# Two cross-attention layers on one core: K's PSUM banks emptied by one ScalarE copy each, masked copies of K made by GpSimd from SBUF

## The chip, the cores and the metric

The kernel runs on one core of a Trainium2 chip. The core's engines run side by side, each through its own queue of instructions: PE (TensorE, the matmuls; PEld is its weight load), DVE (VectorE), ACT (ScalarE), POOL (GpSimd) and SP (SyncE, which issues most DMAs here). They wait for each other through semaphores. The metric is the time of one execution on the device, in microseconds (us).

## The reference

Two layers of multi-head cross-attention, one after the other, each with a residual. There are 32 batch elements with 256 queries of 320 channels, and 77 context rows of 512 channels; 20 heads of 16 channels. All is float32. Further key and value weights of the reference belong to context rows that don't exist in this case, and have no effect.

```python
def layer(x, ctx, Wq, Wk, Wv, Wo, bo):           # x (32, 256, 320), ctx (32, 77, 512)
    q, k, v = heads(x @ Wq), heads(ctx @ Wk), heads(ctx @ Wv)      # 20 heads of 16
    s = einsum('bhqd,bhkd->bhqk', q, k) / sqrt(16)
    o = einsum('bhqk,bhkd->bhqd', softmax(s, axis=-1), v)
    return merge(o) @ Wo + bo + x
x = layer(x, ctx, ...)     # first layer's weights
x = layer(x, ctx, ...)     # second layer's
```

## The kernel before

**Units.** A unit is one layer of one pair of batch elements: 16 pairs x 2 layers = 32 units. Channels lie in the partitions. The 20 heads of the two elements make five groups (g = 0 to 4); in a group, 128 partitions hold four blocks of 32 channels, each of them two heads of 16 (e = 0 and 1). So that one head of a block can be used without its neighbour, K is kept twice, each time with the other head's channels multiplied by zero: `kT[:, e, g]`. `masks` holds the two patterns of ones and zeros. `kM` is kT plus `less`, which puts -1 into one row of the masked half; in the scores that row meets a row of q into which the query's maximum has been written, so that the maximum is subtracted by the matmul itself.

**Steps of a unit.** `keys` and `keys_rest` project K (psk_0 and psk_1 with groups 0 to 3, psk_2 with group 4). `queries` and `queries_rest` project Q, which ACT copies to SBUF; a DMA doubles it (L277). `vals` projects V. `maxima(u, g)` multiplies queries by kT into four banks psm (L326), and DVE takes their maxima (L334); `turn` transposes them and eight DMAs write them into q (L347). `scores(u, g)` multiplies kM by q into four banks pss (L360), and ACT takes the exponential (L366). `products` multiplies by V into po (L380). `divide` transposes po on DVE (L392), takes reciprocals (L396) and normalizes on POOL (`normal`, L401); `turn_back` transposes that on DVE (L415). `finish` and `finish_rest` project the output into psy, and DVE adds bias and residual (L422).

**Order.** The order is written out by hand. Time is cut into slots, five to a unit; unit u's slots begin at s = 5u, and each step is given a slot and a place in it. With u-8 for slot s - 8 and so on, the steps that matter here are:

```python
order = ("load", "maxima", "turn", "scores", "values", "rest", "back", "full", "last")
at(s - 8 if u else s - 9, "rest", lambda u=u: keys(u))
at(s - 7, "rest", lambda u=u: keys_rest(u))
at(s - 5, "rest", lambda u=u: queries_rest(u))
at(s - 6 + g, "maxima", lambda u=u, g=g: maxima(u, g))
at(s + g, "scores", lambda u=u, g=g: scores(u, g))
```

In every slot PE thus does the maxima of one group of a later unit, the scores of one group of the present one, the products of the group before, and then some projection. Each engine runs its instructions in program order.

**Banks.** All matmul outputs come from one pool of eight PSUM banks, `bank(name)`, used in turn: the ninth allocation gets the first one's bank, and its first matmul waits until the last reader of that bank is done. In SBUF, kT and kM have three buffers each (`bufs=3`).

**Who empties K's banks before.** psk_0 and psk_1: one DVE multiply each, which writes both masked copies (L229). psk_2: two ACT activations with the mask as their scale (L253). After these, two POOL additions make kM from kT (L256).

Of the kernel before, what the change touches and what calls it, by code (L numbers as in the profile page):

```python
# [48 lines left out]
F32 = mybir.dt.float32  # L49
AF = mybir.ActivationFunctionType  # L50
ALU = mybir.AluOpType
AX = mybir.AxisListType

B, S, C, CA, L = 32, 256, 320, 512, 77
HEADS, HD = 20, 16
P = 128
# [4 lines left out]
NG = 5  # L61
# [29 lines left out]
def xattn_kernel(ctx: ExitStack, tc: tile.TileContext, xT, cT, cP, weights, outT):  # L91
    nc = tc.nc
# [3 lines left out]
    work = ctx.enter_context(tc.tile_pool(name="work", bufs=3))  # L96
# [6 lines left out]
    def bank(name):  # L103
        return psum.tile([P, 512], F32, tag="bank", name=name)
# [55 lines left out]
    masks = const.tile([P, 2], F32, name="masks")  # L160
    nc.vector.tensor_reduce(masks, r32.rearrange("p (e d) -> p e d", d=HD), AX.X, ALU.add)

    less = const.tile([P, 2], F32, name="less")
# [4 lines left out]
    st = [{} for _ in units]  # L168

    def by_columns(out, lhsT, rhs, **flags):  # L170

        for m in range(0, out.shape[0], 32):
            nc.tensor.matmul(out[m : m + 32], lhsT[:, m : m + 32], rhs, **flags)  # L173

    def of_group(x, g):

        if g < 4:
            return x[:, (g // 2) * NT + (g % 2) * S : (g // 2) * NT + (g % 2 + 1) * S]
        return x[:, 2 * NT : NX]
# [21 lines left out]
    def project_rest(ps, w, w22, x):  # L201

        for kc in range(3):
            for i in range(4):
                b, m = i // 2, i % 2
                r = slice(32 * i, 32 * i + 32)
                if kc < 2:
                    lhsT = w[:, kc, 2 * P + 32 * m : 2 * P + 32 * m + 32]
                    rhs = x[:, kc * NT + b * S : kc * NT + (b + 1) * S]
                else:  # L210
                    lhsT, rhs = w22[:, 0, r], x[:, 2 * NT : NX]
                nc.tensor.matmul(ps[r, 0:S], lhsT, rhs, start=(kc == 0), stop=(kc == 2))  # L212


    def keys(u):
        p, layer = units[u]
        w, c_sb = w_sb[layer], cs[u]
        kT = st[u]["k"] = work.tile([P, 2, NG, L], F32, tag="kT", name=f"kT_{u}", bufs=3)
        for t in range(2):
            ps = bank(f"psk_{u}_{t}")  # L220
            for kc in range(NKA):
                by_columns(
                    ps[:, 0 : 2 * L],
                    w["k"][:, kc, t * P : (t + 1) * P],
                    c_sb[:, kc, :],
                    start=(kc == 0),
                    stop=(kc == NKA - 1),
                )
            nc.vector.tensor_tensor(  # L229
                kT[:, :, 2 * t : 2 * t + 2].rearrange("p e g k -> p e (g k)"),  # L230
                ps[:, 0 : 2 * L].unsqueeze(1).broadcast_to([P, 2, 2 * L]),
                masks.unsqueeze(2).broadcast_to([P, 2, 2 * L]),
                ALU.mult,
            )

    def keys_rest(u):

        p, layer = units[u]
        w, c_sb = w_sb[layer], cs[u]
        kT = st[u]["k"]  # L240
        ps = bank(f"psk_{u}_2")
        for kc in range(NKA):
            for i in range(4):
                b, m = i // 2, i % 2
                nc.tensor.matmul(  # L245
                    ps[32 * i : 32 * i + 32, 0:L],
                    w["k"][:, kc, 2 * P + 32 * m : 2 * P + 32 * m + 32],
                    c_sb[:, kc, b * L : (b + 1) * L],
                    start=(kc == 0),
                    stop=(kc == NKA - 1),  # L250
                )
        for e in range(2):
            nc.scalar.activation(kT[:, e, 4], ps[:, 0:L], AF.Copy, scale=masks[:, e : e + 1])  # L253
        kM = st[u]["km"] = work.tile([P, 2, NG, L], F32, tag="kM", name=f"kM_{u}", bufs=3)
        for e in range(2):
            nc.gpsimd.tensor_scalar_add(kM[:, e], kT[:, e], less[:, e : e + 1])  # L256

    def queries(u):
        p, layer = units[u]
# [10 lines left out]
    def queries_rest(u):  # L270
        p, layer = units[u]
        w = w_sb[layer]
        q0, q1 = st[u]["q"]
        ps = bank(f"psq_{u}_2")
        project_rest(ps, w["q"], w["q22"], xs[p])
        nc.scalar.copy(of_group(q0, 4), ps[:, 0:S])
        nc.sync.dma_start(out=q1, in_=q0)  # L277

    def load_chunk(layer, i):
        n = min(P, B * L - i * P)  # L280
        c_sb = cvs[layer, i] = io.tile([P, NKA, P], F32, tag="cv", name=f"cv_{layer}_{i}", bufs=3)
        nc.sync.dma_start(out=c_sb[:, :, :n], in_=cT[:, :, i * P : i * P + n])
# [170 lines left out]
    for u, (p, layer) in enumerate(units):  # L453
# [3 lines left out]
        if u > 0:  # L457
            at(s - 12, "load", lambda u=u: load_context(u))
        at(s - 8 if u else s - 9, "rest", lambda u=u: keys(u))
        at(s - 9, "last", lambda u=u: queries(u))  # L460
        at(s - 7, "rest", lambda u=u: keys_rest(u))
        need = range(p * NB * L // P, ((p + 1) * NB * L - 1) // P + 1)
        when = s - 6
        for i in need:
# [6 lines left out]
            made[layer] += 1  # L471
            when = s - 5
        at(s - 5, "rest", lambda u=u: queries_rest(u))
        for g in range(NG):
            at(s - 6 + g, "maxima", lambda u=u, g=g: maxima(u, g))
# [121 lines left out]
```

## Time and profile before

| | |
|---|---|
| median of 3 runs | 999.02 us (992.94 to 1000.55) |
| the profiled execution's own time | 995.15 us |
| its span, first to last instruction | 993.4 us |
| PE busy | 977.5 us, 98% |
| DVE busy | 590.9 us, 59% |
| ACT busy | 421.7 us, 42% |
| POOL busy | 182.7 us, 18% |
| DVE multiply from psk_0, psk_1 (L229) | 64 instructions, 479 ns each |
| ACT activation from psk_2 (L253) | 64 instructions, 322 ns each |
| POOL addition for kM (L256) | 64 instructions, 1260 ns each |

Busy times are unions over the whole span, so PE's 98% says that nearly always some matmul is under way, not that matmuls follow one another as closely as they could. In rows of the profile, "kT<-psk,masks" is an instruction that writes kT and reads psk and masks; buffer numbers are left out. In the timeline the columns are start, duration, engine, line, operation, tiles and shapes, count, and in brackets the engine's idle time ahead of the group with what ended it. In a table by stretch of time the columns are the stretch, its length, and each engine's busy time with the number of instructions, then the granted PE clock, the DMA share and GB/s.

### The profile page before, as it was taken

The numbers are of one execution on the slowest core, as the hardware profiler recorded it, in microseconds if no ns is written. First come the engines' busy times: TensorE is split into PE (matmuls) and PEld (weight loads), VectorE is DVE, ScalarE is ACT, GpSimd is POOL, SyncE is SP. The second block draws the span as 40 slices with busy tenths as digits, with TensorE's granted clock in tenths as the row PEclk, the third lists the DMA queues.
The fourth block names the chain that finished last, engine by engine and source line by source line (L and its number), as shares of the span: only waits on it lengthen the run. The fifth ranks groups of instructions, "written<-read, shape, count | busy, mean of one in ns | idle before, by whom it ended". The sixth has DMA issues, their size and how long they took to land.

```text
span 993.4 us, 43878 instructions
## 1 busy us (share of the span) xinstructions
PE 977.5 (98%) x19664; PEld 609.0 (61%) x19664; DVE 590.9 (59%) x1380; ACT 421.7 (42%) x905; POOL 182.7 (18%) x236
## 2 busy tenths in 40 slices
PE   7899999999999999999999999999999999999988
PEld 4566665666666666665666666666666666666644
DVE  2466555666655665655666656666556656556654
ACT  1344343454444443444444444444444534444442
POOL 2122201221202222112222112221022221122211
PEclk9999999999999999999999999999999999999989
DMA  6541222221132411223212232311323111231111
GB/s 213 177 160 37 74 79 97 70 77 62 57 122 70 132 47 60 92 80 122 71 44 85 68 123 70 122 34 53 121 80 119 50 62 54 69 107 48 58 47 54
DMA packets 53949, 83.59 MB, mean 84 GB/s; under 512 B 15556, under 2 KB 35652, under 8 KB 53762
## 3 DMA queue, kind: packets, MB, share of 16 engines
q1 hardware_dynamic: 53330, 78.96, 23.9%
q8 instruction: 154, 2.52, 1.0%
q10 hardware_dynamic: 432, 1.84, 0.5%
q14 instruction: 33, 0.27, 0.1%
HBM read 35.39 MB, written 10.49 MB: 46 GB/s over the span
## 4 chain that ended last, share of the span: by engine, by line
PE 97%; DVE 1%; DMA 1%; SPq 1%; issue 0%; POOL 0%; DVEq 0%; POOLq 0%
PE po L380 16%; PE pss L360 15%; PE psy L173 14%; PE psq L173 14%; PE psm L326 12%; PE psv L173 8%; PE psk L173 7%; PE psq L212 4%; PE psy L212 4%; PE psk L245 2%; SPq L347 1%; DVE max L334 1%; DMA w<-in_w_dram 0%; DMA q<-mT 0%; DVE mT L343 0%
## 5 line engine op out<-in xcount | busy, mean ns | idle before, releaser
L366 ACT ACTIVATE pT<-pss 77x512 f32<-77x512 f32 x640 | 326.9, 590 | 242.1 <-PE pss L360 242.1
L334 DVE TENSOR_REDUCE max<-psm 128x4 f32<-128x308 f32 x640 | 259.4, 466 | 172.1 <-PE psm L326 172.1
L401 POOL TENSOR_TENSOR normal<-turned,inv 128x256 f32<-128x256 f32 x160 | 99.3, 621 | 763.9 <-DVE inv L396 763.9
L360 PE MATMUL pss<-q,kM 32*77 32x256 f32 x2560 | 180.6, 380 | 5.8 <-DMA q<-mT 5.8
L380 PE MATMUL po<-pT,v 77*32 77x256 f32 x2560 | 174.0, 389 | 1.0 <-DVE max L334 1.0
L173 PE MATMUL psy<-oT,w 128*32 128x256 f32 (+1 forms) x3072 | 149.4, 380 | 0.0
L173 PE MATMUL psq<-x,w 128*32 128x256 f32 (+1 forms) x3072 | 149.4, 380 | 0.0
L392 DVE STREAM_TRANSPOSE turned<-po 128x512 f32<-128x512 f32 x160 | 113.3, 708 | 46.0 <-PE po L380 42.9
L268 ACT COPY q<-psq 128x256 f32<-128x256 f32 x128 | 47.6, 372 | 213.3 <-PE psq L173 209.5
L326 PE MATMUL psm<-kT,q 32*128 32x154 f32 x2560 | 129.1, 314 | 0.0
L360 PEld LDWEIGHTS pss<-q,kM 32*77 32x77 f32 x2560 | 114.4, 142 | 23.4 <-issue 10.6
L326 PEld LDWEIGHTS psm<-kT,q 32*128 32x128 f32 x2560 | 91.9, 183 | 55.3 <-issue 41.7
L380 PEld LDWEIGHTS po<-pT,v 77*32 77x32 f32 x2560 | 67.5, 110 | 90.3 <-DVE max L334 58.4
L415 DVE STREAM_TRANSPOSE oT<-normal 128x256 f32<-128x256 f32 x160 | 70.9, 443 | 84.5 <-POOL normal L401 81.4
L173 PEld LDWEIGHTS psq<-x,w 128*32 128x32 f32 (+1 forms) x3072 | 85.4, 109 | 57.6 <-issue 14.4
L173 PEld LDWEIGHTS psy<-oT,w 128*32 128x32 f32 (+1 forms) x3072 | 82.2, 108 | 61.2 <-issue 13.2
L422 DVE SCALAR_TENSOR_TENSOR x<-psy,w,x 128x256 f32<-128x256 f32 x160 | 68.6, 479 | 62.8 <-PE psy L173 56.4
L173 PE MATMUL psv<-w,cv 128*32 128x320 f32 x1232 | 93.5, 433 | 0.0
L256 POOL TENSOR_SCALAR kM<-kT,less 128x385 f32<-128x385 f32 x64 | 79.9, 1260 | 38.8 <-ACT kT L253 38.6
L173 PE MATMUL psk<-c,w 128*32 128x154 f32 x2048 | 75.2, 299 | 5.6 <-DMA w<-in_w_dram 5.6
L173 PEld LDWEIGHTS psk<-c,w 128*32 128x32 f32 x2048 | 67.0, 112 | 12.8 <-DMA w<-in_w_dram 5.6
L173 PEld LDWEIGHTS psv<-w,cv 128*32 128x32 f32 x1232 | 41.0, 110 | 40.6 <-issue 1.9
(24 smaller groups left out, 328.3 us busy)
## 6 DMA issues: line engine op xcount, KB each, us to landing
q<-q SPq DMA_DIRECT2D x32, 640.0 KB
x<-in_xT_dram SPq DMA_DIRECT2D x16, 640.0 KB
c<-in_cP_dram SPq DMA_DIRECT2D x32, 308.0 KB
cv<-in_cT_dram SPq DMA_DIRECT2D x38, 256.0 KB
out_dram<-x SPq DMA_DIRECT2D x15, 640.0 KB
v<-stage SPq DMA_DIRECT2D x26, 192.5 KB
q<-mT SPq DMA_DIRECT2D x256, 5.0 KB
w<-in_w_dram ACTq DMA_DIRECT2D x2, 640.0 KB
```

The source lines that it names most:

```text
L173: nc.tensor.matmul(out[m : m + 32], lhsT[:, m : m + 32], rhs, **flags)
L212: nc.tensor.matmul(ps[r, 0:S], lhsT, rhs, start=(kc == 0), stop=(kc == 2))
L256: nc.gpsimd.tensor_scalar_add(kM[:, e], kT[:, e], less[:, e : e + 1])
L326: nc.tensor.matmul(ps[j][:, c * 2 * L : (c + 1) * 2 * L], q[r, c * P : (c + 1) * P], kT[r, :, g, :], start=True, stop=True,)
L334: nc.vector.tensor_reduce(mx[:, 2 * g : 2 * g + 2, 2 * j : 2 * j + 2], ps[j][:, : 4 * L].rearrange("p (c e k) -> p c e k", e=2, k=L), AX.X ...
L360: nc.tensor.matmul(ps[j][:L, e * S : (e + 1) * S], kM[r, e, g, :], q[r, :], start=True, stop=True,)
L366: nc.scalar.activation(st[u]["p", g][j][:L], ps[j][:L], AF.Exp, scale=SCALE)
L380: nc.tensor.matmul(po[32 * j : 32 * j + 32, e * S : (e + 1) * S], vpad[:L, b, pair, e].rearrange("p a d -> p (a d)"), pT[j][:L, e * S : (e ...
L392: nc.vector.transpose(turned[:, 0 : 2 * S], po)
L401: nc.gpsimd.tensor_tensor(normal.rearrange("p q e d -> p e q d"), outs, inv.unsqueeze(3).broadcast_to([P, 2, S // 32, HD]), ALU.mult,)
L415: nc.vector.transpose(of_group(st[u]["o"], g), normal)
L422: nc.vector.scalar_tensor_tensor(x, ps[:, 0:S], w_sb[layer]["b"][:, 0, t : t + 1], x, ALU.add, ALU.add)
```

## The change

One new tile, kR (two buffers), holds K unmasked. psk_0, psk_1 and psk_2 are each read by one plain ACT copy into kR. POOL multiplies kR by the masks into kT: groups 0 to 3 with two instructions in slot u-8, group 4 with two in slot u-7. kM is made from kR by POOL, with a multiplication and an addition in one instruction, two instructions, and this step moves from the end of `keys_rest` (slot u-7) to the end of `queries_rest` (slot u-5). No matmul and no DMA changes, nor their order. Lines of code behind the change move down by nine, so L360 becomes L369 and so on.

```diff
+    def mask_keys(u, g0, g1):
+        kR, kT = st[u]["kr"], st[u]["k"]
+        for e in range(2):
+            nc.gpsimd.tensor_scalar_mul(kT[:, e, g0:g1], kR[:, g0:g1], masks[:, e : e + 1])
+
+    def less_keys(u):
+        kR = st[u].pop("kr")
+        kM = st[u]["km"] = work.tile([P, 2, NG, L], F32, tag="kM", name=f"kM_{u}", bufs=3)
+        for e in range(2):
+            nc.gpsimd.tensor_scalar(
+                kM[:, e], kR, masks[:, e : e + 1], less[:, e : e + 1], ALU.mult, ALU.add
+            )
+
     def keys(u):
...
-        kT = st[u]["k"] = work.tile([P, 2, NG, L], F32, tag="kT", name=f"kT_{u}", bufs=3)
+        kR = st[u]["kr"] = work.tile([P, NG, L], F32, tag="kR", name=f"kR_{u}", bufs=2)
+        st[u]["k"] = work.tile([P, 2, NG, L], F32, tag="kT", name=f"kT_{u}", bufs=3)
...
-            nc.vector.tensor_tensor(
-                kT[:, :, 2 * t : 2 * t + 2].rearrange("p e g k -> p e (g k)"),
-                ps[:, 0 : 2 * L].unsqueeze(1).broadcast_to([P, 2, 2 * L]),
-                masks.unsqueeze(2).broadcast_to([P, 2, 2 * L]),
-                ALU.mult,
-            )
+            nc.scalar.copy(kR[:, 2 * t : 2 * t + 2].rearrange("p g k -> p (g k)"), ps[:, 0 : 2 * L])
+        mask_keys(u, 0, 4)
...
     def keys_rest(u):
...
-        for e in range(2):
-            nc.scalar.activation(kT[:, e, 4], ps[:, 0:L], AF.Copy, scale=masks[:, e : e + 1])
-        kM = st[u]["km"] = work.tile([P, 2, NG, L], F32, tag="kM", name=f"kM_{u}", bufs=3)
-        for e in range(2):
-            nc.gpsimd.tensor_scalar_add(kM[:, e], kT[:, e], less[:, e : e + 1])
+        nc.scalar.copy(st[u]["kr"][:, 4], ps[:, 0:L])
+        mask_keys(u, 4, 5)
...
     def queries_rest(u):
...
         nc.sync.dma_start(out=q1, in_=q0)
+        less_keys(u)
```

More of the change, by code (lines that the diff above doesn't have):

```diff
@@ L239, in keys_rest @@
         w, c_sb = w_sb[layer], cs[u]
-        kT = st[u]["k"]
         ps = bank(f"psk_{u}_2")
```

## The prediction

> **What bounds the kernel now.** I read the page first, for the engine that is full; then the table of waits, for what that engine still waits for; then the timeline of the ten microseconds around the keys of one unit; and last the busy time of the score matmuls, slot by slot.
>
> The page shows one full engine and a chain that stays on it:
>
> ```profile
> PE 977.5 (98%) x19664; PEld 609.0 (61%) x19664; DVE 590.9 (59%) x1380; ACT 421.7 (42%) x905; POOL 182.7 (18%) x236
> PE 97%; DVE 1%; DMA 1%; SPq 1%; issue 0%; POOL 0%; DVEq 0%; POOLq 0%
> ```
>
> DVE, which the change relieves, is busy 59% and carries 1% of the chain. In the table of waits, PE's own lines come to 12.4 us:
>
> ```profile
> PE pss L360 <- DMA q<-mT: 5.8, 4, 1.7
> PE psk L173 <- DMA w<-in_w_dram: 5.6, 1, 5.6
> PE po L380 <- DVE max L334: 1.0, 2, 0.8
> ```
>
> None of them is a wait for K. But a PE that is always "busy" can still be held up: matmuls overlap, so one that starts late only makes its group longer. So I compared equal groups. In the steady state a unit takes 29.63 us and has five groups of 16 score matmuls (pss, L360), with equal shapes. The busy time of pss in the stretch from each group's start to that of the group behind it, over one unit:
>
> ```profile
> 502.69:503.66 0.97, 0.97 (x16) 0.48 (x16) 0.00 (x0) 1.00 0.00 0
> 507.39:508.45 1.06, 1.06 (x16) 0.68 (x16) 0.00 (x0) 1.00 0.00 0
> 511.91:513.07 1.16, 1.16 (x16) 0.67 (x16) 0.04 (x1) 1.00 0.06 9
> 516.86:517.86 1.00, 1.00 (x16) 0.57 (x16) 0.00 (x0) 1.00 0.80 246
> 520.79:521.76 0.97, 0.97 (x16) 0.48 (x16) 0.00 (x0) 1.00 0.07 26
> ```
>
> The second column is the length, the next the PE busy time with the number of matmuls. Same work, but 0.97, 1.06, 1.16, 1.00 and 0.97 us. The two long ones follow the key projections (psk). The timeline tells why:
>
> ```profile
> 506.90 0.48 DVE L229 TENSOR_TENSOR kT<-psk,masks 128x308 f32<-128x308 f32 x1 [0.50 <-PE psk L173]
> 507.39 1.12 PE L360 MATMUL pss<-q,kM 32*77 32x256 f32 x16
> 510.83 0.62 POOL L401 TENSOR_TENSOR normal<-turned,inv 128x256 f32<-128x256 f32 x1 [4.26 <-DVE inv L396]
> 511.28 0.81 PE L326 MATMUL psm<-kT,q 32*128 32x154 f32 x16
> 511.47 0.54 ACT L253 ACTIVATE kT<-psk,masks 128x77 f32<-128x77 f32 x2 [0.91 <-POOL normal L401]
> 511.89 2.50 POOL L256 TENSOR_SCALAR kM<-kT,less 128x385 f32<-128x385 f32 x2 [0.44 <-ACT kT L253]
> 511.91 1.23 PE L360 MATMUL pss<-q,kM 32*77 32x256 f32 x16
> ```
>
> PSUM's eight banks go round in order of allocation. Counting eight on from psk_1 (psm 4, pss 4) gives the fourth bank of the next slot's scores; the same count leads from psk_2 to the fourth bank one slot later. psk_1 is read by DVE until 506.90 + 0.48 = 507.38, just when the scores start (507.39); the fourth score matmul's weight load is due ahead of that. psk_2 is read by two ACT instructions until 511.47 + 0.54 = 512.01, while its successor's scores start at 511.91. Both times the fourth score matmul comes late, 0.09 and 0.19 us for the group. That is what this change can win on PE, and nothing else in the unit is tied to K.
>
> **What the Trainium skill says.** "ScalarE: Activation LUTs", section "What ACT_TABLE_LOAD costs", gives 0.833 ns per element and about 93 ns more for each pointer operand. The trace agrees: copies of 256 and 320 elements take 372 and 425 ns (53/64 = 0.83 ns), while L253, with its mask as a pointer, takes 322 ns for 77. "GPSIMD Engine Reference", section 4.1, says that GpSimd has no way into PSUM, hence the copy first, and that one-input operations run roughly at line rate; here kM's 385 elements take 1260 ns, 3.3 ns each. "SBUF — State Buffer", section "Who interferes with whom", says that a DVE instruction with at most one SBUF input, outside the two-port modes, does not contend with GpSimd. The case agrees: the 64 kM instructions all lasted 1258 to 1266 ns, beside whatever DVE did.
>
> **The change part by part.**
>
> *Bank of psk_1 (slot u-8).* Two DVE multiplies of 479 ns go, two ACT copies of 154 elements come. Their length: 372 - 102 x 0.83 = 287 ns, an estimate from the copy row. ACT has finished its exponentials at 505.85 and next has work at 508.51, so the copy starts where DVE's multiply did, 506.90, and the bank is free at 507.19 instead of 507.38: 0.20 us before the scores. The 0.09 us go. Bounds: 0 to 0.09; I take 0.09, since the copy could be 0.1 us longer and still be early.
>
> *Bank of psk_2 (slot u-7).* Two ACT instructions (0.54 us together) become one plain copy of 77: 372 - 179 x 0.83 = 223 ns. Free at 511.47 + 0.22 = 511.69 instead of 512.01, and the scores start at 511.91. The 0.19 us go. Bounds: 0.15 to 0.19.
>
> *kT now comes from POOL.* The first maxima of the unit read kT at 511.28. POOL has its slot's `normal` until 505.95 + 0.62 = 506.57; the second copy ends at 507.19; POOL starts 0.10 us after ACT ends (511.79 to 511.89 at kM). Two multiplies of 308: 308/385 x 1.26 = 1.01 us each, so 507.29 + 2.02 = 509.31. Hidden by 1.97 us of PE work ahead of 511.28. Behind the masks in POOL's queue is the next `normal` (510.83), for which DVE's turn_back waits: 1.5 us to spare. Group 4's two masks start near 511.8 and even at kM's price end at 514.3, before `normal` at 515.37; their reader comes over 20 us later. Cost nothing.
>
> *kM moved to slot u-5.* Two instructions of 1.26 us, behind `normal` (520.15 + 0.62 = 520.77): end 523.29, next `normal` 524.04. The form has two operations now, which no row shows; between 1.26 and 2.52 us each. Even at 2.52 (end 525.81) only one turn_back is 1.8 us late, in the slot where DVE's next work is the residual sum of 526.92, and whose product isn't read in that slot. The scores that read kM are a unit away. The step stands behind the issue of the q copy on SP in program order, but issues no DMA: SP's queue keeps its order.
>
> *DVE loses 2 x 0.48 us a unit.* Off the path: nothing. The maxima of that slot start earlier, which nobody waits for.
>
> *Waits added.* The maxima of groups 0 and 4 wait for DVE and POOL instead of DVE alone. The group of scores with most waits (516.86) is 0.03 us longer than the shortest, so 0 to 0.03 each, 0 to 1.8 us over 60; kM's scores lose their POOL waits in exchange. I take 0.3.
>
> *Start.* The second unit's maxima follow its keys by a short slot (psk ends 30.96, psm at 32.30); masks from POOL would be ready at about 30.96 + 0.07 (DVE's start there) + 0.29 + 0.10 + 2.02 = 33.4, a stall of 1.2 us. PE waits 1.49 us for the q DMA at 37.62, which hangs on the maxima before it, so the stall vanishes there.
>
> *Sum.* Units 2 to 31 have both long groups: 30 x (0.09 + 0.19) = 8.4, less 0.3: 8.1 us. On the profiled execution's 995.15 us (span 993.4 and 1.75 around it) that is 987.0. The median of the three runs, 999.02, lies 3.9 us above that execution; the four times shown (992.94, 995.15, 999.02, 1000.55) have a mean of 996.9, and I count from there: 988.8. About 1% is what a measurement of this kernel can tell from no change, and 988.8 lies 1.0% below the median.
>
> **The rivals.**
> - *Only psk_2's wait goes.* The ACT copy takes longer to start or run than DVE's multiply did, and psk_1's bank is late as before: 30 x 0.19 - 0.3 = 5.4, so 991.5. Against it: 0.20 us of slack.
> - *More goes.* The group at 58.09 lasts 1.50 us, and is followed by 0.23 us of waiting for DVE's max; a lighter DVE could mend both (0.7), and dropped waits the 0.03 of thirty groups (0.9): about 987.
> - *Nothing is left of it.* The time saved is lost again at the end, where the last units wait for DMAs (5.8 us) and the page shows the clock down to 8 tenths in one slice; or the next bank in the round is late. 996.9.
> - *Slower: the first maxima wait for POOL.* If the multiply ran at twice kM's price per element, 2.02 us, the masks would end at 511.33 and PE would hardly notice; from about 2.1 us each the stall exceeds the 0.28 won. At 2.52 each they end at 512.33, PE goes on 0.1 later: 1.15 us x 30 = 34.5, less 8.4: 1023. Against it: `normal`, a multiply of two inputs, takes 621 ns for 256, so multiplying isn't dear on POOL.
>
> **How the numbers follow.** Both waits gone: 0.70, of which 0.45 over 1% faster, since a median of three has been as high as 999 and the forecast lies on the bound. Only psk_2: 0.11 (0.03 faster). More: 0.08, faster. Nothing left: 0.06. POOL late: 0.05. Faster 0.56, same 0.39, slower 0.05. The range, 982 to 996, is the forecast with the 7.6 us spread of the runs and the first two rivals; it leaves out POOL late and most of "nothing left".
>
> **What would show it.** Right: the five groups at 0.97, 0.97, 0.97, 1.00, 0.97; a unit of 29.35 us; POOL's masks near 1.0 us, ended 2 us ahead of the maxima. Wrong: psm waiting for POOL's kT, a pss group still at 1.06, or a unit of 29.6 us or more.

## The result, and the profile after

The changed kernel takes 988.55 us (median of 14 runs, 984.77 to 992.31), the kernel before 994.62 us (median of 14, 992.84 to 1000.55). The ratio is 0.9919, with a 95% interval of 0.9901 to 0.9938: 0.8% faster, within the 1% that the prediction called about what one measurement can tell. It is not the quotient of the two medians, which are 6.07 us apart (0.9939). The profiled execution took 986.19 us, with a span of 984.4 us; before it was 995.15 and 993.4.

The page still shows a full PE, and the chain still lies on it:

```profile
PE 968.2 (98%) x19664; PEld 597.3 (61%) x19664; DVE 566.7 (58%) x1316; ACT 430.1 (44%) x937; POOL 240.9 (24%) x364
PE 97%; DMA 1%; DVE 1%; SPq 1%; POOL 0%; issue 0%; ACT 0%; DVEq 0%; POOLq 0%
```

The share alone would say that nothing happened: 98% before and after. What moved is the length of the matmul groups. This is the busy time of pss, stretch by stretch over one unit of the changed kernel, for the same five groups of scores that the prediction showed (in such rows for pss the engines are PE, PEld and ACT):

```profile
499.63:500.60 0.97, 0.97 (x16) 0.48 (x16) 0.00 (x0) 1.00 0.00 0
504.33:505.30 0.97, 0.97 (x16) 0.49 (x16) 0.00 (x0) 1.00 0.00 0
508.76:509.74 0.98, 0.97 (x16) 0.49 (x16) 0.00 (x0) 1.00 0.06 9
513.52:514.52 1.00, 1.00 (x16) 0.57 (x16) 0.00 (x0) 1.00 0.87 292
517.45:518.42 0.97, 0.97 (x16) 0.48 (x16) 0.00 (x0) 1.00 0.07 26
```

The second group went from 1.06 to 0.97 us and the third from 1.16 to 0.97 (0.98 is the rounding of the stretch's ends). The other three are as they were. The timeline of the same unit shows the banks coming free in time:

```profile
503.84 0.29 ACT L245 COPY kR<-psk 128x154 f32<-128x154 f32 x1 [0.71 <-PE psk L173]
504.23 2.08 POOL L219 TENSOR_SCALAR kT<-kR,masks 128x308 f32<-128x308 f32 x2 [0.72 <-ACT kR L245]
504.33 1.04 PE L369 MATMUL pss<-q,kM 32*77 32x256 f32 x16
507.74 0.62 POOL L410 TENSOR_TENSOR normal<-turned,inv 128x256 f32<-128x256 f32 x1 [1.44 <-DVE inv L405]
508.13 0.81 PE L335 MATMUL psm<-kT,q 32*128 32x154 f32 x16
508.27 0.22 ACT L263 COPY kR<-psk 128x77 f32<-128x77 f32 x1 [0.78 <-PE psk L256]
508.76 1.04 PE L369 MATMUL pss<-q,kM 32*77 32x256 f32 x16
```

psk_1's bank is free at 503.84 + 0.29 = 504.13, 0.20 us ahead of its scores; psk_2's at 508.49, 0.27 us ahead. POOL's masks end at 506.31, well ahead of `normal` (507.74) and of the first maxima (508.13).

The wait itself shows in the weight loads (PEld). These two stretches end where the first score matmul behind psk_2 starts, in the kernel before and in the one after:

```profile
511.77:511.91 0.14, 0.00 (x0) 0.13 (x3) 0.00 (x0) 1.00 0.17 28
```

```profile
508.63:508.76 0.13, 0.00 (x0) 0.12 (x4) 0.00 (x0) 1.00 0.09 14
```

After the change all four first loads, one for each bank, have started by then. Before it only three have; the fourth waits for ACT's semaphore in the trace and starts at 512.06, 0.05 us behind the end of psk_2's last reader (512.01).

Between the V projection that starts at 60.71 us in the kernel before (61.53 after) and the maxima that start at 948.57 (941.34 after), PE does the same matmuls in both, for 29 units' keys. This middle part took 887.86 us and now takes 879.80: 8.06 us less, 0.278 us for each of the 29. The rest of the 9.0 us by which the two spans differ comes from both ends. There single executions differ even of the same kernel: over 35 executions of the kernel before in a later series, the mean granted PE clock goes from 0.988 to 0.997. One sees it in the granted PE clock (the number behind POOL's) of such stretches, first of the kernel before, then of the one after:

```profile
40.00:43.50 3.50, 3.50 (x63) 2.24 (x63) 0.75 (x2) 2.30 (x5) 0.00 (x0) 1.00 0.38 113
962.60:972.80 10.20, 10.20 (x88) 3.87 (x88) 2.83 (x6) 5.50 (x11) 1.24 (x2) 0.50 0.12 47
```

```profile
40.00:43.50 3.50, 3.50 (x37) 1.62 (x36) 0.00 (x0) 2.42 (x5) 0.00 (x0) 0.52 0.34 105
954.80:961.70 6.90, 6.35 (x56) 2.45 (x56) 1.42 (x3) 3.37 (x7) 0.62 (x1) 0.51 0.24 97
```

At both places PE waits for q's DMAs, and in three of the four rows it gets half its clock for some microseconds; how many differs among the traces of this study (none, 3.4 or 6.8 us in the first 65 us, 3.4 to 20.5 us at the end). The kernels below therefore are compared by their middle part as well as by their times. Its start and end are the same two instructions in every trace.

### The profile page after: what moved, and what is told of

Its sections match the earlier page's. It is cut to its first block, busy times and chain, and to the rows that moved or that the text cites. A ratio compares the mean times of both kernels' runs of the same rounds, so it can differ in the third digit from the quotient of the medians.

```text
span 984.4 us, 43943 instructions
## 1 busy us (share of the span) xinstructions
PE 968.2 (98%) x19664; PEld 597.3 (61%) x19664; DVE 566.7 (58%) x1316; ACT 430.1 (44%) x937; POOL 240.9 (24%) x364
## 3 DMA queue, kind: packets, MB, share of 16 engines
q8 instruction: 154, 2.52, 1.0%
## 4 chain that ended last, share of the span: by engine, by line
PE 97%; DMA 1%; DVE 1%; SPq 1%; POOL 0%; issue 0%; ACT 0%; DVEq 0%; POOLq 0%
PE po L389 16%; PE psy L173 15%; PE psq L173 15%; PE pss L369 14%; PE psm L335 12%; PE psv L173 9%; PE psk L173 7%; PE psq L212 4%; PE psy L212 4%; PE psk L256 2%; SPq L356 1%; DMA w<-in_w_dram 1%; DVE max L343 0%; DMA q<-mT 0%; POOL kT L219 0%
## 5 line engine op out<-in xcount | busy, mean ns | idle before, releaser
L369 PE MATMUL pss<-q,kM 32*77 32x256 f32 x2560 | 170.9, 377 | 4.5 <-DMA q<-mT 4.5
L369 PEld LDWEIGHTS pss<-q,kM 32*77 32x77 f32 x2560 | 102.2, 142 | 24.5 <-issue 6.8
L219 POOL TENSOR_SCALAR kT<-kR,masks 128x77 f32<-128x77 f32 (+1 forms) x128 | 96.7, 766 | 50.9 <-ACT kR L245 41.3
```

The lines of the kernel that those rows point to most:

```text
L219: nc.gpsimd.tensor_scalar_mul(kT[:, e, g0:g1], kR[:, g0:g1], masks[:, e : e + 1])
L369: nc.tensor.matmul(ps[j][:L, e * S : (e + 1) * S], kM[r, e, g, :], q[r, :], start=True, stop=True,)
```

## The experiments

The theory: the fourth score matmul of a group waits for the last reader of psk_1's or psk_2's bank, and an earlier release is the whole gain. The rival: DVE was relieved of 0.96 us a unit, and that is what helped. A second rival: POOL's new load takes something back.

**Groups 0 to 3 alone.** The two copies from psk_0 and psk_1 and POOL's masks for them; psk_2 and kM as before.

```diff
-            nc.vector.tensor_tensor(kT[...], ps[...], masks[...], ALU.mult)
+            nc.scalar.copy(kR[:, 2 * t : 2 * t + 2].rearrange("p g k -> p (g k)"), ps[:, 0 : 2 * L])
+        mask_keys(u, 0, 4)
```

> The change for groups 0 to 3 only: psk_0 and psk_1 by ACT copies and POOL masks; psk_2 and kM as before. Bank theory: the score group after psk_0/psk_1 shortens from 1.06 to 0.97, the one after psk_2 stays at 1.16; a steady unit of 29.54 us; 30 x 0.09 = 2.6 us faster in the steady part, less the stall of about 1.2 us at the second unit's first maxima, which may return at the wait for the q DMA: ratio 0.997 to 0.999. Rival (a lighter DVE is what helps, bank or no bank): nearly the whole gain of the change, ratio about 0.992 and both groups shorter.

Measured: ratio 0.9974 [0.9954, 0.9994]; middle part 883.98 us, 3.88 less than before. From the timeline of this kernel:

```profile
506.73 1.04 PE L363 MATMUL pss<-q,kM 32*77 32x256 f32 x16
510.67 0.54 ACT L256 ACTIVATE kT<-psk,masks 128x77 f32<-128x77 f32 x2 [0.78 <-PE psk L248]
511.17 1.18 PE L363 MATMUL pss<-q,kM 32*77 32x256 f32 x16
```

The first of the two groups is short, as the theory has it (1.12 to 1.04 us of overlapping busy time), and DVE's relief didn't shorten the other to the same length. But that one didn't stay where it was either: 1.18 instead of 1.23. ACT's two activations last 0.54 us as before, and start 0.05 us earlier after psk_2. In the kernel before they waited for DVE, PE and POOL, of which a separate instruction in ACT's queue took a part; here kT's other writer is POOL, and they wait for PE alone. So the release came 0.05 us earlier and the group got 0.05 us shorter. (The prediction's timeline names POOL's `normal` as what released them. It was another: at 481.83 us of the kernel before they start while `normal` still runs, until 482.10.)

**Group 4 alone.** psk_2 by one copy, two masks on POOL, kM from kT in the old place, psk_0 and psk_1 by DVE.

```diff
-        for e in range(2):
-            nc.scalar.activation(kT[:, e, 4], ps[:, 0:L], AF.Copy, scale=masks[:, e : e + 1])
+        kR = work.tile([P, L], F32, tag="kR", name=f"kR_{u}", bufs=2)
+        nc.scalar.copy(kR, ps[:, 0:L])
+        for e in range(2):
+            nc.gpsimd.tensor_scalar_mul(kT[:, e, 4], kR, masks[:, e : e + 1])
```

> The change for group 4 only: psk_2 by one ACT copy, its two masks by POOL; psk_0 and psk_1 by DVE as before; kM stays where it was. Bank theory: the group after psk_2 shortens from 1.16 to 0.97, the one after psk_0/psk_1 stays at 1.06; a steady unit of 29.44 us; 30 x 0.19 = 5.7 us faster, ratio 0.994, and no stall at the second unit's maxima. Rival (lighter DVE): DVE has all its work here, so no gain, ratio 1.000.

Measured: ratio 0.9954 [0.9938, 0.9969]; middle part 882.30, 5.56 less than before, or 0.19 us for each of 29 units. The two groups in its timeline:

```profile
505.62 1.12 PE L362 MATMUL pss<-q,kM 32*77 32x256 f32 x16
510.14 1.04 PE L362 MATMUL pss<-q,kM 32*77 32x256 f32 x16
```

Each half of the change mends its own group, and DVE, which here has all its work, is no hindrance to 5.56 us of the gain. The two halves add up to more than 8.06 (3.88 + 5.56 = 9.44), because 0.05 us a unit of the first half lies in the group that the second mends: 29 x 0.05 = 1.4. kM stays in slot u-7 in both, so its move to u-5 has no part in the gain.

**DVE refilled.** The changed kernel with two DVE multiplies per unit in the old place of the queue, written to a tile that nobody reads.

```diff
         mask_keys(u, 0, 4)
+        for t in range(2):
+            nc.vector.tensor_tensor(
+                idle[:, :, 0 : 2 * L],
+                r32[:, 0:1].unsqueeze(1).broadcast_to([P, 2, 2 * L]),
+                masks.unsqueeze(2).broadcast_to([P, 2, 2 * L]), ALU.mult,
+            )
```

> The changed kernel with DVE given back the work it lost: in each unit two multiplies of 308 elements at the old place in DVE's queue, which read constants and write a tile that nobody reads. Bank theory: no effect on PE, unit 29.36 us, ratio to the kernel before 0.991 to 0.993 as the change itself. Rival (lighter DVE): the gain is lost, ratio 0.998 to 1.000.

Measured: ratio 0.9917 [0.989, 0.9945]; middle part 879.82, the changed kernel's 879.80 again. The timeline shows the work present and the groups short:

```profile
502.40 1.22 DVE L249 TENSOR_TENSOR idle<-r,masks 128x308 f32<-128x308 f32 x2
504.08 1.04 PE L377 MATMUL pss<-q,kM 32*77 32x256 f32 x16
508.51 1.04 PE L377 MATMUL pss<-q,kM 32*77 32x256 f32 x16
```

The first rival falls: 1.22 us of DVE work in this unit, more than the 0.96 that were taken away, costs nothing.

**The bank held.** The changed kernel with a second ACT reader of psk_2 behind the copy.

```diff
         nc.scalar.copy(st[u]["kr"][:, 4], ps[:, 0:L])
+        nc.scalar.activation(idle, ps[:, 0:L], AF.Copy, scale=masks[:, 0:1])
```

> The changed kernel with a second ACT reader of psk_2 behind the copy, an activation with the mask as scale into a tile nobody reads, so that the bank comes free later and nothing else changes. The runs so far: the last reader ended 13 ns before the score group's start (group 86 ns longer), 46 ns after it (145), 95 ns after it (192), 205 ns before it (0): 98 ns plus the offset. Here copy and activation end about 508.72 on the changed kernel's clock, 40 ns before the group's start at 508.76: the group after psk_2 is 0.05 to 0.06 us longer than in the changed kernel, 1.03 us, once a unit, and the unit 29.41. If only a bank held past the start of the group costs anything: 0.97 and 29.36.

One execution with its profile: 990.58 us, middle part 881.32, 1.52 more than the changed kernel, 0.052 for each of 29 units.

```profile
508.73 0.23 ACT L264 COPY kR<-psk 128x77 f32<-128x77 f32 x1 [0.78 <-PE psk L257]
508.85 0.33 ACT L265 ACTIVATE idle<-psk,masks 128x77 f32<-128x77 f32 x1
509.23 1.09 PE L371 MATMUL pss<-q,kM 32*77 32x256 f32 x16
```

The last reader ends at 509.18, 0.05 us before the group begins, and the group is still 0.05 us longer. This was foretold from the four releases seen before it. In these groups each nanosecond by which the bank comes free later than 98 ns before the first matmul makes the group about one nanosecond longer.

None of these releases lies between 0.05 and 0.2 us before the start, but the unit has one more bank that does, and it explains the group of 1.00 us. Eight banks ahead of that group's fourth bank lies V's projection (psv), which ACT copies. In the changed kernel:

```profile
513.03 0.42 ACT L306 COPY stage<-psv 128x320 f32<-128x320 f32 x1 [1.10 <-PE psv L173]
513.52 1.07 PE L369 MATMUL pss<-q,kM 32*77 32x256 f32 x16
```

The copy ends at 513.45, 0.07 us before the group; the fourth weight load waits for ACT and starts at 513.50, and the group is 0.03 us longer than the shortest, as the releases above would have it (98 - 68 = 30 ns). So it is with 35 groups of the middle part, in the kernel before and in the changed one: about 1 us of the same loss is left. No kernel here frees V's bank sooner to test that. Groups whose bank was free 0.11 us ahead or more have no loss (0.97 us).

**Masks made twice.** The changed kernel with the multiplies of groups 0 to 3 doubled, to see where POOL's margin ends.

```diff
-            nc.gpsimd.tensor_scalar_mul(kT[:, e, g0:g1], kR[:, g0:g1], masks[:, e : e + 1])
+            for _ in range(2 if g0 == 0 else 1):
+                nc.gpsimd.tensor_scalar_mul(kT[:, e, g0:g1], kR[:, g0:g1], masks[:, e : e + 1])
```

> The changed kernel with each mask multiply of groups 0 to 3 made twice, four POOL instructions of 1.05 us instead of two. In the changed kernel they start at 504.23 and the first maxima at 508.13; four of them end at 508.4 and PE goes on 0.1 later. Bank theory with POOL's margin of 1.8 us: the first maxima of each unit are 0.35 to 0.4 us late, so the gain of 0.28 a unit is more than lost: unit 29.7 us, ratio 1.001 to 1.005. In the second unit the stall grows from 1.2 to 3.3 us. If POOL's masks have more margin than that, or PE waits for something else, no loss: ratio 0.992.

Measured: 1006.75 us, ratio 1.0108 [1.0061, 1.0155]; middle part 895.24, 7.4 more than before and 15.4 more than the changed kernel.

```profile
514.99 4.39 POOL L220 TENSOR_SCALAR kT<-kR,masks 128x308 f32<-128x308 f32 x4 [0.72 <-ACT kR L246]
519.34 0.62 POOL L411 TENSOR_TENSOR normal<-turned,inv 128x256 f32<-128x256 f32 x1
519.43 0.81 PE L336 MATMUL psm<-kT,q 32*128 32x154 f32 x16 [0.46 <-POOL kT L220]
```

PE now waits for POOL's kT, 0.53 us a unit (15.4/29). The direction was foretold and the size was not: 0.35 to 0.4 was said. The four multiplies took 4.39 us, not 4 x 1.05 = 4.2, and the start of the program lost 3.3 us against the changed kernel (its V projection starts at 64.85 us, against 61.53): PE waits 1.76 us for the third unit's masks at 60.73, and its clock is halved for another 3.4 us from 61.07. This is the prediction's slower rival made real, and it shows that the change is safe by 1.8 us of POOL time and no more.

**Two-operation masks.** The changed kernel with POOL's multiply in the form that kM has.

```diff
-            nc.gpsimd.tensor_scalar_mul(kT[:, e, g0:g1], kR[:, g0:g1], masks[:, e : e + 1])
+            nc.gpsimd.tensor_scalar(
+                kT[:, e, g0:g1], kR[:, g0:g1], masks[:, e : e + 1], masks[:, e : e + 1],
+                ALU.mult, ALU.mult,
+            )
```

> The changed kernel with each mask multiply written as two operations, times mask and times mask again, the form in which kM's instruction took 660 ns for 385 elements where the addition alone had taken 1260. If the form sets the price, the masks of 308 elements take about 0.55 us instead of 1.05 and those of 77 about 0.25 instead of 0.48. PE waits for no mask in the steady part, so the unit stays at 29.36 us and the ratio at 0.991 to 0.993; the second unit's first maxima stall 0.2 instead of 1.2 us, which the next wait for the q DMA swallows in either case. Rival (POOL's load is what still costs, through turn_back and DVE): a shorter unit, ratio 0.990 or less.

Measured: ratio 0.9924 [0.9906, 0.9941]; middle part 879.80. POOL's groups, first of the changed kernel, then of this one:

```profile
L219 POOL TENSOR_SCALAR kT<-kR,masks 128x308 f32<-128x308 f32 x64 | 66.5, 1049 | 41.3 <-ACT kR L245 41.3
L226 POOL TENSOR_SCALAR kM<-kR,masks,less 128x385 f32<-128x385 f32 x64 | 41.8, 660 | 0.0
L219 POOL TENSOR_SCALAR kT<-kR,masks 128x77 f32<-128x77 f32 x64 | 30.2, 484 | 9.6 <-ACT kR L263 9.6
```

```profile
L219 POOL TENSOR_SCALAR kT<-kR,masks 128x308 f32<-128x308 f32 x64 | 37.7, 598 | 41.3 <-ACT kR L248 41.3
L219 POOL TENSOR_SCALAR kT<-kR,masks 128x77 f32<-128x77 f32 x64 | 25.5, 408 | 10.9 <-ACT kR L266 10.9
```

The masks take 63.2 us of POOL instead of 96.7, and the middle part is the same to 0.01 us: POOL's load takes nothing back, so the second rival falls. The version is no faster than the change, but its masks end 0.9 us earlier, and so leave a wider margin.

**kM's form alone.** The kernel before, with kM made from kT by two operations.

```diff
-            nc.gpsimd.tensor_scalar_add(kM[:, e], kT[:, e], less[:, e : e + 1])
+            nc.gpsimd.tensor_scalar(
+                kM[:, e], kT[:, e], masks[:, e : e + 1], less[:, e : e + 1], ALU.mult, ALU.add
+            )
```

> The kernel before with nothing changed but the form of kM's instruction: kT times mask plus less, instead of kT plus less. Same input, same place. If the form sets the price, 660 ns instead of 1260; if the input or the place set it in the changed kernel, it stays at 1260. On time: no effect, since nobody waits for kM: ratio 0.999 to 1.001, score groups 1.06 and 1.16 as before.

Measured: ratio 1.0002 [0.9987, 1.0017]; middle part 887.91 against 887.86. Its kM:

```profile
L256 POOL TENSOR_SCALAR kM<-kT,masks,less 128x385 f32<-128x385 f32 x64 | 41.9, 666 | 40.4 <-ACT kT L253 40.4
```

1260 became 666 ns with the same kT in the same place, so it is the form (a second operation, with a second scalar for each partition) that sets the price; and 38 us less of POOL work over the run moved the time by nothing.

## Why the prediction was right, point by point

- **psk_1's bank.** Said: copy of 287 ns, free 0.20 us before the scores, 0.09 us gained a unit. Measured: 288 ns, 0.20 us, 1.06 to 0.97. Right.
- **psk_2's bank.** Said: copy of 223 ns, 0.19 us gained. Measured: 224 ns, 1.16 to 0.97. Right in size; but the release came at 0.27 us before the group instead of 0.22. The working left the start of ACT's work where it was, and missed that with PE alone to wait for it starts 0.05 us earlier. Where the copy had POOL to wait for as well (group 4 alone), the bank came free 0.22 us before the group, as said.
- **Masks on POOL.** Said: 1.01 us each, done 1.97 us before the maxima, 1.5 us before `normal`. Measured: 1.05 us, 1.82 and 1.43. Right.
- **kM.** Said: between 1.26 and 2.52 us. Measured: 0.66. The term was mis-sized, and its lower bound was wrong: a second operation was taken to cost time or nothing, and the form with two is the cheaper one. As kM is off the path, the sum doesn't feel it.
- **DVE.** Said: nothing. Shown by the kernel with DVE refilled.
- **Added waits.** Said: 0.3 us lost. The middle part gained 29 x 0.278 = 8.06 us, what the two groups alone give (0.086 + 0.192 us by the trace's instructions): nothing was lost. The 0.03 us were read wrongly: the prediction put the group of 1.00 us down to its number of waits, but it is V's bank that comes late there, and the 7 of the 35 such groups in which PE has no separate instruction to wait are as long as the others.
- **The start.** Said: a stall of 1.2 us at the second unit's first maxima, which the next wait for q's DMA swallows. In the trace after, PE waits 1.18 us for POOL's kT there, and the wait ahead of the first scores shrinks from 1.49 to 0.23 us, which start at 37.30 instead of 37.62 (the maxima ahead of the stall already at 27.60 instead of 27.91). Right. The 0.8 us by which the V projection at 60.71 comes later in that trace belongs to the half-clock stretch at 40 us: from the second half of those scores to it, the kernel before takes 20.82 us (39.89 to 60.71) and the changed one 21.98; the kernel with only kM's form changed has half a clock there too, and takes 21.99 without any such stall, while the changed kernel with DVE refilled has the stall but the full clock, and takes 20.83.
- **The sum.** Said: 8.1 us for 30 units, 988.8. Measured: 8.06 us for the 29 units of the middle part, for which the prediction's terms give 29 x 0.27 = 7.8. The terms are right, but that 988.55 lies so near to 988.8 is luck, for two misses cancel. The base was 2.3 us too high: the prediction counted from 996.9, the mean of four times, and over 14 runs the median is 994.62 (in two later series it was 997.10 and 997.02). And the two medians lie 6.07 us apart, 2.0 less than 8.1, as far as the traces tell because the ends of the program differ from execution to execution. The prediction gave more chance to "over 1% faster" than to "within 1%" on the strength of a median of three that was high, 999.02; 8.1 us of 995 is 0.8%.
- **The rivals.** Only psk_2's wait goes: no, though the kernel that does just that took what was reckoned for it, 5.56 us in the middle (5.7 before the waits were taken off). More goes: no, the group of 1.00 stayed at 1.00, and the group at 58.09 with the wait behind it takes 1.79 us (58.86 to 60.65) instead of 1.73. Nothing is left: no, the middle part keeps all that the two groups give, and the stretch behind it is not longer (43.0 us, against 44.8). Slower: not here, but the doubled masks reach it.

## What to carry to other kernels

A full engine can still be held up: compare groups of equal work; here the 9 to 20% by which two of them were longer led to a wait that the table of idle time didn't show. With banks that go round, count on from a bank to its next user; the last reader's end against that user's start is the price. Here a plain copy to SBUF, with the arithmetic afterwards on an engine that had time, released the banks sooner than arithmetic straight from PSUM (0.29 us instead of 0.48, 0.22 instead of 0.54). Before work is put on a slow engine, work out when the first reader wants it: here the margin was 1.8 us, and doubling the work turned 0.8% faster into 1.1% slower.

## What the runs showed of the hardware that was not expected

- GpSimd's `tensor_scalar` with per-partition scalars was cheaper with two operations than with one: 660 against 1260 ns for 385 float32 elements, 598 against 1049 for 308, 408 against 484 for 77. From 77 to 308 elements that is 0.82 ns for each element more (190/231), against 2.4 (565/231).
- A score matmul whose bank came free less than about 0.1 us before its group started delayed the group. Last reader's end 110 ns or more before the start: nothing lost; 68 ns before it (V's bank), 29 ns; 44 ns before it (the bank held), 53; 13 ns before it, 86; 46 ns after it, 145; 95 ns after it, 192.
- ACT's first reader of psk_2 started 66 ns after PE's last matmul where it waited for PE alone. Where it waited for more engines, and a separate instruction in ACT's queue took a part of the waits, it started 115 ns (DVE, PE and POOL) or 119 ns (PE and POOL) after it.
